# A four-layer network on one core: where three sets of small steps are issued, and which engine does two steps of layer 0's scan

## The chip, the core and the metric

The kernel runs on one core of one Trainium2 chip. It is launched once for a whole forward pass. The metric is device time in microseconds (us), the median of the timed runs. Beside it stands one execution taken by the hardware profiler, with a record for each instruction of the tensor engine (PE, with its weight loads as PEld), the vector engine (DVE), the scalar engine (ACT), GpSimd (POOL) and for the DMA issues of SyncE (SP).

## What is computed

The input is four images of 96 channels, 128 x 128 pixels, in float32. Four layers follow each other, each with a group normalisation ahead of it and its input added behind it:

```python
x = x + _L0_conv_ref(_gn(x), ...)   # conv, two selective scans (forward and backward), layer norm, gate, projection
x = x + _L1_conv_ref(_gn(x), ...)   # local conv, fractional Fourier and FFT branches, 3x3 conv
x = x + _L2_conv_ref(_gn(x), ...)   # deformable 3x3 conv (gathers)
x = x + _L3_conv_ref(_gn(x), ...)   # DCT, layer norm, four Mamba blocks of 16 states, inverse DCT
```

In layer 0 each of the two scans runs over the 16,384 pixels as `h = exp(delta*A)*h + delta*B*u` and gives `y = C*h + D*u`. The results of both directions are added; the sum is normalised over its 96 channels (mean taken off, divided by the root of the mean square), multiplied by a gate and projected. In layer 3 every quadrant of the transformed image goes through the same kind of recurrence with 16 states for each of 192 inner channels.

## The kernel before, in words

The program goes through the samples in phases (`tile_net_kernel`, loop over `b` from -1 to 4, lines 2053 to 2070). A phase has two lanes of work, `front` of sample b+1 (layers 0 and 1 and the offsets of layer 2) and `back` of sample b (the gathers of layer 2 and the head of layer 3), and the inverse transform of sample b-1 beside the front. After them stands `layer3(b)` alone, the Mamba scans. So the profile has one front alone (0 to about 1,630 us), three pairs of a mixed phase and a layer 3, a phase with the back and the inverse alone, and the last layer 3.

Front and back are recorded by a planner (`Program`, line 238). It lists each lane's operations, plans them with rough costs, and issues them so that the two lanes advance in proportion to their plans. While a lane is in layer 0's scan its plan is compressed (`self.program.pace = 0.1`, line 688), so that the other lane does little then. Layer 3 has a planner of its own (`Order`, line 419): an operation is added with an engine, a cost, a key and the operations that it follows; the planner takes the earliest start and, among those that could start within 0.12 us of it, the lowest key. Either way each engine's instructions end in one fixed order (`InOrder`, line 56, ties them), and each engine works through its list strictly in that order. The lists record nearly all operations through one helper, so the profile puts them at L66 (L403 for DMAs), and the reader goes by the names of the tiles (the first letters of a layer's prefix and the digit are cut: `l0_ct` and `l3_ct` are both `l_ct`).

DMAs are issued by SP, one after the other, each where its wait ends. GpSimd issues the gathers of layer 2 (`DMA_INDIRECT l_g<-quad_d,l_i`).

The start. `scan_constants` (line 1540) is called ahead of everything. It loads layer 3's vectors (`l3_vec`) and decay logs (`l3_Alog` into `al`, eight partitions by 16 states to a DMA), then makes `al = -exp(al)`, two columns `rest` and a selection matrix `pick`. Layer 0 then loads its weights and the image in eight pieces (`l0_xt`, line 628) for the normalisation's statistics, and convolves block by block.

Layer 0's scan (`scan`, line 692). A step is a tile of 96 x 512 in one direction k. Steps go forward and backward in turn, n from 0 to 31 for each direction. In the first half (n < 16) a step ends with its `C*h` stored to `part_d`. In the second half the other direction's part is loaded (`part`), and the step goes on (line 754 on): three matmuls into `pm` (the skip term `uc`, `part`, `h`, each through the centring matrix), ACT squares `pm` into `sq` and copies it into `ct`, PE averages the squares into `pv`, ACT makes the inverse root, DVE multiplies, ACT applies the affine, DVE multiplies by the gate, PE projects into `po`, DVE adds the input and takes statistics. `pm`, `pv` and `po` share two PSUM banks (tag "a"). Ahead of all that GpSimd multiplies `du` by the step size `dl`, the only thing that it does in a step.

Layer 3 (`layer3`, line 1503). Two quadrants side by side make a half (`qh` 0 and 1); each half has eight tiles of 512 pixels, so there are 16 tiles i, and each tile has 48 recurrences (`DB` multiplies on DVE, `SC` scans on DVE, `HC` multiplies on GpSimd, ...). `pick2`, a second selection matrix, is filled by two DVE instructions ahead of the planner. For the first tile of a half `pair_head` (line 1638) adds eight operations `weights0` to `weights7`: the generator `pair_weights` (line 1583) issues 34 weight DMAs on SP and prepares them on DVE (`wc` by `win`, copies into `wx`, the split of `wdt` into `wh` and `wl`). The tile's own data (`xc`, DMA from `xd_d`) is loaded by the operation `load`, which follows `weights7`. Then come the layer norm (`pm`, `sub`, `sq`, `pv`, `ln`, `root`, `mul`, `aff`), the convolution (`pu`), the gate (`pz`), the projection (`pb`) and the recurrences. The weights of the second half have nothing to wait for, so the planner issues them right behind those of the first.

Of the kernel before, what the change touches and what calls it, by code (L numbers as in the profile page):

```python
# [23 lines left out]
F32 = mybir.dt.float32  # L24
# [22 lines left out]
def lanes(ap, n):  # L47

    return ap.unsqueeze(2).to_broadcast([ap.shape[0], ap.shape[1], n])
# [452 lines left out]
class Net:  # L502
# [107 lines left out]
    def layer0(self, xin, T, beside):  # L610
# [3 lines left out]
        with self.program.pool(name="l0w", bufs=1) as wp, self.program.pool(name="l0p", bufs=1, space=PSUM) as ps:  # L614
# [74 lines left out]
            with self.program.pool(name="l0b", bufs=3) as wb:  # L689
                edges = [None, None]  # L690

                def scan(k, n):
# [62 lines left out]
                    nc.tensor.matmul(out=pm, lhsT=center[:, 1, :], rhs=uc, start=True, stop=False)  # L755
                    nc.tensor.matmul(out=pm, lhsT=center[:, 0, :], rhs=part, start=False, stop=False)
                    nc.tensor.matmul(out=pm, lhsT=center[:, 0, :], rhs=h, start=False, stop=True)
                    yield
                    ct = wb.tile([C, CH], F32, name="l0_ct", tag="ct")
                    sq = wb.tile([C, CH], F32, name="cn_s", tag="sq")  # L760
                    nc.scalar.activation(sq, pm, AF.Square)
                    nc.scalar.copy(ct, pm)
                    yield
                    pv = ps.tile([C, CH], F32, name="cn_v", tag="a", bufs=2)
# [738 lines left out]
    def layer3(self, T):  # L1503
        tc, nc = self.tc, self.nc
        T.yd_d = self.plane("yd_d")
        with tc.tile_pool(name="l3w", bufs=1) as wp, tc.tile_pool(name="l3q", bufs=2) as wq, tc.tile_pool(
            name="l3p", bufs=2, space=PSUM
        ) as ps, tc.tile_pool(name="l3b", bufs=2) as wb:
            self.pick2 = wp.tile([128, 32, 2, 64], F32R, name="pick2")
            for q in range(2):  # L1510
                nc.vector.tensor_tensor(
                    self.pick2[:, :, q, :],
                    lanes(self.ident[:, 32 * q : 32 * q + 32], 64),
                    lanes(self.ident[:, 64 + 32 * q : 96 + 32 * q], 64),
                    ALU.add,
                )
# [23 lines left out]
    def scan_constants(self, pool):  # L1540


        nc, a = self.nc, self.a
        self.al = pool.tile([128, 2, 3, DS], F32, name="l3_al")
        self.vec = pool.tile([128, 2, 3, 3], F32, name="l3_vec")
        for qh in range(2):
            for j in range(3):
                for q, p, n, m, c in self.inner_parts(j):
                    nc.sync.dma_start(
                        out=self.vec[p : p + n, qh, j, :], in_=a["l3_vec"][c : c + n, 2 * qh + q, m, :]  # L1550
                    )
                    for i in range(0, n, 8):
                        g = (m * C + c + i) // 8
                        nc.sync.dma_start(
                            out=self.al[p + i : p + i + 8, qh, j, :],
                            in_=a["l3_Alog"][2 * qh + q][:, g].rearrange("(e s) -> e s", s=DS),
                        )
        al = self.al.rearrange("p h j s -> p (h j s)")
        nc.scalar.activation(al, al, AF.Exp)
        nc.vector.tensor_scalar_mul(al, al, -1.0)  # L1560


        self.rest = pool.tile([64, 2], F32, name="rest")
        nc.vector.memset(self.rest[:, 0:1], 1.0)
        nc.vector.memset(self.rest[:, 1:2], 0.0)
        for r in (12, 44):
            nc.sync.dma_start(out=self.rest[r : r + 12, 1:2], in_=a["k_ones"][0:12, 0:1])
        nc.vector.tensor_tensor(
            self.rest[:, 0:1], self.rest[:, 0:1], self.rest[:, 1:2], ALU.subtract
        )  # L1570
        self.pick = pool.tile([128, 64], F32R, name="pick")
        nc.vector.tensor_tensor(self.pick, self.ident[:, 0:64], self.ident[:, 64:128], ALU.add)
# [10 lines left out]
    def pair_weights(self, qh, wq):  # L1583
# [7 lines left out]
        wo = wq.tile([128, 3, C], F32, name="l3_wo", tag="wo")  # L1591
        wdt = wq.tile([64, 3, 128], F32, name="l3_wdt", tag="wdt", bufs=1)
        nc.gpsimd.memset(wdt, 0.0)
        for q in range(2):
            nc.sync.dma_start(out=win[:, q, :], in_=a["l3_winT"][2 * qh + q][:, 0 : 2 * C])
            nc.sync.dma_start(out=wz[:, q, :], in_=a["l3_winT"][2 * qh + q][:, 2 * C : 4 * C])
            nc.sync.dma_start(
                out=wc[:, q], in_=a["l3_cwT"][2 * qh + q].unsqueeze(0).to_broadcast([C, 4, 2 * C])
            )
        for j in range(3):  # L1600
            for q, p, n, m, c in self.inner_parts(j):
                nc.sync.dma_start(out=xp[p : p + n, j, :], in_=a["l3_xpT"][2 * qh + q][c : c + n, m, :])
                nc.sync.dma_start(out=wo[p : p + n, j, :], in_=a["l3_woT"][2 * qh + q][c : c + n, m, :])
# [6 lines left out]
        yield 3.0  # L1610
        for q in range(2):
            nc.vector.tensor_tensor(
                wc[:, q], wc[:, q], win[:, q].unsqueeze(1).to_broadcast([C, 4, 2 * C]), ALU.mult
            )
            yield 1.0

        wx = wq.tile([128, 3, 96], F32, name="l3_wx", tag="wx")
        nc.gpsimd.memset(wx, 0.0)
        for j in range(3):
            for q, p, n, _ in self.PARTS[j]:  # L1620
                nc.vector.tensor_copy(wx[p : p + n, j, 32 * q : 32 * q + 32], xp[p : p + n, j, R6:])
                for d in range(2):
                    o = 64 + 12 * d + R6 * q
                    nc.vector.tensor_copy(wx[p : p + n, j, o : o + R6], xp[p : p + n, j, 0:R6])
            yield 0.5

# [5 lines left out]
        nc.vector.tensor_tensor(wl, wdt, whf, ALU.subtract)  # L1632
        yield 1.0
        nc.vector.tensor_scalar(wl, wl, self.rest[:, 1:2], 0.0, ALU.mult, ALU.add)
# [3 lines left out]
    def pair_head(self, i, at, T, before, wq, wb, ps, order):  # L1638
# [11 lines left out]
        T.px = slice(qh * HW * W + t * 2 * CH, qh * HW * W + (t + 1) * 2 * CH)  # L1650
        if t == 0:
            weights = self.pair_weights(qh, wq)

            def more():
                T.wts = next(weights)

            T.wts = None
            for k in range(8):
                o("DVE", 1.0, more, f"weights{k}", after=[f"weights{k - 1}"] if k else [])

        def load():
# [10 lines left out]

        o("DVE", 0.2, load, "load", after=["weights7"] if t == 0 else [],
          others=([last.ops["aff1"]] if last else []) + used("pz2", 2) + used("out", 3))

        def norm(h):
# [47 lines left out]
        norm(1)  # L1724
        ready = ["aff0", "aff1"]
        v = SimpleNamespace(pu={}, pz={})
# [76 lines left out]
        def bc_low():  # L1803
            nc.vector.tensor_tensor(T.bc[64:128, :], v.pb[0:64, :], T.bc[0:64, :].bitcast(F32), ALU.subtract)

        for j in range(3):
            o("PE", 0.9, partial(proj, j), f"pb{j}", after=["silu"] if j == 0 else [f"pb{j - 1}"],
              opens="pb" if j == 0 else None)
# [93 lines left out]
    def pair_scans(self, xd_d, yd_d, wq, wb, ps):  # L1902
# [13 lines left out]

        carry = {}

        def scans(i, T):
# [7 lines left out]
            for n in range(48 * i, 48 * i + 48):  # L1927
# [55 lines left out]
                free = lambda k: ("E", n - k)  # L1983
                pC = main("PC", n, "PE", 0.36, pc, -5.2, (H("bc"), 0), ("PC", n - 1), ("CS", n - 1))
                dA = main("DA", n, "ACT", 0.69, da, -5.1, (H(f"dl{j}"), 0), ("DA", n - 1), ("SC", n - AHEAD))
                main("CS", n, "ACT", 0.58, cs, -5.0, ("PC", n), ("CS", n - 1), ("HC", n - AHEAD))
                pB = main("PB", n, "PE", 0.36, pb, -1000.0, (H("bc"), 0), ("PB", n - 1), ("DB", n - 2))
                dB = main("DB", n, "DVE", 0.62, db, 0.0, ("PB", n), (H(f"du{j}"), 0), ("DB", n - 1), ("SC", n - 2))
# [25 lines left out]

        both(0)
        for i in range(len(tiles)):
            scans(i, parts[i])
            if i + 1 < len(tiles):
                both(i + 1)
# [4 lines left out]
def kernel(ctx: ExitStack, tc: tile.TileContext, a: dict, out: bass.AP):  # L2024
# [5 lines left out]
    net.constants(const)  # L2030
    net.scan_constants(const)
    program = net.program
    net.smalls = [program.pool(f"small{lane}", 1) for lane in range(2)]
# [19 lines left out]
    for b in range(-1, n + 1):  # L2053
# [13 lines left out]
        program.end()  # L2067
        net.nc = net.engines
        if 0 <= b < n:
            net.layer3(samples[b])  # L2070
# [153 lines left out]
```

## Time and profile before

| what | value |
|---|---|
| median of 3 timed runs | 18,809.84 us (18,797.6 to 18,822.2) |
| the profiled execution, whole | 17,757.5 us |
| its span, first to last instruction | 17,755.7 us |
| mean granted PE clock in it | 0.899 |
| busy: PE / DVE / ACT / POOL | 14,126.8 / 12,556.5 / 11,138.5 / 10,731.0 us |
| first image DMA of layer 0 issued | 82.03 us |
| first scan step of layer 0: front alone, then the three mixed phases | 410.1, 2,167.6, 6,408.0, 10,595.9 us |
| last tile of that scan added | 748.8, 2,530.3, 6,753.6, 10,940.4 us |
| first DMA of layer 3 (`l_ln`), four samples | 4,051.8, 8,237.0, 12,423.1, 15,936.2 us |

How to read it: a group's line in the profile gives the engine, the operation and the tiles as output<-inputs, then a count and durations. A line of the timeline gives start and duration in us, merged where equal instructions follow each other; in square brackets stands how long the engine was idle before it and what ended that. In a table of windows each engine's busy time in a stretch is followed by its count of instructions, and the last columns are the PE clock, the share of the DMA engines and GB/s. A float32 matmul has two records, one for each pass. An engine's busy time is no bound by itself; what counts is what is late next in the stretch concerned.

### The profile page before, as it was taken

What the parts mean: (1) busy time and instruction counts of PE and PEld (TensorE: products, weight loads), DVE (VectorE), ACT (ScalarE), POOL (GpSimd) and SP (SyncE); (2) the same over time, 40 slices, a digit from 0 to 9 for tenths busy, and PEclk for the clock granted to TensorE, in tenths of its full rate; (3) what the DMA queues carried; (4) which work ended last, traced back from release to release, by engine and by line L of the source; (5) the groups of instructions that cost most, each with busy time, mean ns of one, the idle gap of its engine ahead of it and who ended that gap; (6) DMA issues with size and microseconds to landing.
All of it is one profiled execution on the core that took longest, in us unless ns stands there. A gap on an engine that the chain in (4) does not pass through costs nothing. (4 is left out here: it accounts for less than half of the span.)

```text
span 17755.7 us, 171824 instructions
## 1 busy us (share of the span) xinstructions
PE 14126.8 (80%) x41152; PEld 6431.4 (36%) x41152; DVE 12556.5 (71%) x22642; ACT 11138.5 (63%) x24735; POOL 10731.0 (60%) x9556
## 2 busy tenths in 40 slices
PE   7897887888998787888999788788899842248998
PEld 2263334433333332634333332444333321123333
DVE  1725585677999576567999757567899855558997
ACT  1613675556777576555777567554777656547776
POOL 0102635636888645553888764562788877747887
PEclk9998998989999897988999898898999966579999
DMA  3525656661000757563000476666000165540001
GB/s 80 159 82 162 182 171 185 190 188 37 8 9 7 208 172 210 172 185 118 9 8 8 118 205 180 182 193 185 11 8 8 35 184 159 158 127 6 8 9 48
DMA packets 1189540, 1940.84 MB, mean 109 GB/s; under 512 B 191985, under 2 KB 711601, under 8 KB 1169457
## 3 DMA queue, kind: packets, MB, share of 16 engines
q1 hardware_dynamic: 893616, 1023.60, 19.9%
q0 software_dynamic: 294912, 906.26, 17.6%
q8 instruction: 328, 5.37, 0.1%
q14 instruction: 684, 5.60, 0.1%
HBM read 1473.67 MB, written 455.61 MB: 109 GB/s over the span
## 5 line engine op out<-in xcount | busy, mean ns | idle before, releaser
L66 POOL DMA_INDIRECT l_g<-quad_d,l_i x4608 | 4552.4, 988 | 3454.4 <-issue 1218.2
L66 ACT ACTIVATE l_acc<-l_g,l_v 128x96 f32<-128x96 f32 x9216 | 3170.0, 344 | 2599.8 <-DVE l_part L66 1557.3
L66 POOL TENSOR_TENSOR l_hc<-l_h,l_cs 128x512 f32<-128x512 f32 x3072 | 3854.5, 1274 | 846.3 <-PE l_py L66 271.4
L66 DVE TENSOR_TENSOR_SCAN l_h<-l_dA,l_carry,l_dB 128x512 f32<-128x512 f32 x3072 | 3916.2, 1275 | 165.8 <-ACT l_carry L66 73.9
L66 ACT ACTIVATE l_dA<-l_dl,l_al 128x512 f32<-128x512 f32 x3072 | 2182.9, 722 | 807.5 <-DVE l_h L66 806.7
L66 DVE SCALAR_TENSOR_TENSOR l_sm<-l_g,l_v,l_acc 128x96 f32<-128x96 f32 x4608 | 1408.1, 312 | 1693.4 <-ACT l_acc L66 1552.0
L66 PE MATMUL l_py<-l_hc,ident 128*128 128x512 f32 x4608 | 2386.6, 607 | 20.0 <-POOL l_hc L66 11.6
L66 DVE TENSOR_TENSOR l_dB<-l_du,l_pB 128x512 f32<-128x512 f32 x3072 | 2135.7, 695 | 317.0 <-POOL l_du L66 25.9
L66 PE MATMUL l_pt<-ident,l_sm 128*128 128x128 f32 (+1 forms) x3584 | 793.9, 329 | 1829.3 <-ACT l_acc L66 706.6
L66 PE MATMUL l_pB<-l_bc,pick 128*128 128x512 f32 x3072 | 1774.8, 578 | 561.5 <-DVE l_dB L66 530.4
L66 ACT COPY l_cs<-l_pC 128x512 f32<-128x512 f32 x3072 | 1782.9, 580 | 626.9 <-PE l_pC L66 541.1
L66 DVE SCALAR_TENSOR_TENSOR l_part<-l_g,l_v,l_acc 128x96 f32<-128x96 f32 x4608 | 1428.0, 310 | 1021.2 <-ACT l_acc L66 1009.7
L66 PE MATMUL l_pC<-l_bc,pick 128*128 128x512 f32 x3072 | 1546.7, 503 | 113.6 <-ACT l_cs L66 104.1
L66 PEld LDWEIGHTS l_pt<-ident,l_sm 128*128 128x128 f32 (+1 forms) x3584 | 507.3, 164 | 2459.8 <-ACT l_acc L66 1432.6
L66 PEld LDWEIGHTS l_pB<-l_bc,pick 128*128 128x128 f32 x3072 | 581.1, 189 | 2215.7 <-DVE l_dB L66 2117.7
L66 PE MATMUL l_pc<-rows,l_wc 96*96 96x508 f32 (+2 forms) x2304 | 1101.3, 611 | 5.8 <-DVE rows L66 5.8
L66 PE MATMUL l_p<-rows,l_c 96*96 96x508 f32 (+2 forms) x2304 | 1078.3, 609 | 30.6 <-DMA rows<-cat_d 14.8
L66 POOL TENSOR_TENSOR l_du<-l_du,l_dl 96x512 f32<-96x512 f32 x256 | 329.3, 1287 | 1263.9 <-DVE l_dl L66 841.6
L66 PE MATMUL l_pu<-l_xq,l_wc 96*64 96x512 f32 (+1 forms) x2048 | 1079.1, 617 | 13.6 <-ACT l_xq L66 13.6
L66 PE MATMUL l_pc<-l_sT,l_wk 128*96 128x512 f32 (+1 forms) x1792 | 1005.7, 676 | 53.1 <-ACT l_sT L66 53.1
L66 PEld LDWEIGHTS l_py<-l_hc,ident 128*128 128x128 f32 x4608 | 879.9, 193 | 381.9 <-issue 172.7
L66 POOL TENSOR_TENSOR l_hc<-l_hc 128x512 f32<-128x512 f32 x768 | 978.0, 1273 | 55.2
(253 smaller groups left out, 21354.0 us busy)
## 6 DMA issues: line engine op xcount, KB each, us to landing
quad_d<-l_qt SPq DMA_DIRECT2D x124, 768.0 KB
x<-l_x SPq DMA_DIRECT2D x384, 192.0 KB
l_g<-quad_d,l_i POOLq DMA_INDIRECT x4608
mix<-l_mx SPq DMA_DIRECT2D x256, 256.0 KB
sp_in<-mix SPq DMA_DIRECT2D x256, 256.0 KB
l_uc<-u_d SPq DMA_DIRECT2D x256, 192.0 KB
l_x<-x SPq DMA_DIRECT2D x256, 192.0 KB
l_xs<-x SPq DMA_DIRECT2D x116, 256.0 KB
```

The source lines that it names most:

```text
L66: ins = op(*args, **kw).ins
```

## The change

It has three parts.

1. Layer 0's scan. The matmul of `part` is gone; GpSimd adds `part` to `h`, and one matmul takes the sum. ACT's square of `pm` is gone; GpSimd squares the copy `ct`.
2. The start. The 12 loads of `l3_vec` and 96 of `l3_Alog` are issued by GpSimd instead of SP. `al`, `rest` and `pick` are made in a function of their own, `scan_lines`, called after the first front has been issued.
3. Layer 3's head. `load` comes first; the weights follow it, in six operations instead of eight, their DMAs in another order (`win`, `wc`, `wz`, `xp`, `wdt`, `wo`), and only what needs them waits for them. The second half's weights now follow the second half's `load`. `pick2` is filled by two operations of the planner, which follow `sub0` and `sub1` of the first tile.

```diff
 # layer 0, scan
                     nc.tensor.matmul(out=pm, lhsT=center[:, 1, :], rhs=uc, start=True, stop=False)
-                    nc.tensor.matmul(out=pm, lhsT=center[:, 0, :], rhs=part, start=False, stop=False)
+                    nc.gpsimd.tensor_tensor(h, h, part, ALU.add)
+                    yield
                     nc.tensor.matmul(out=pm, lhsT=center[:, 0, :], rhs=h, start=False, stop=True)
...
-                    nc.scalar.activation(sq, pm, AF.Square)
                     nc.scalar.copy(ct, pm)
+                    nc.gpsimd.tensor_tensor(sq, ct, ct, ALU.mult)
 # scan_constants
-                    nc.sync.dma_start(
+                    self.tc.nc.gpsimd.dma_start(
                         out=self.vec[p : p + n, qh, j, :], in_=a["l3_vec"][c : c + n, 2 * qh + q, m, :]
...
-                        nc.sync.dma_start(
+                        self.tc.nc.gpsimd.dma_start(
                             out=self.al[p + i : p + i + 8, qh, j, :],
...
+    def scan_lines(self, pool):
+        nc, a = self.nc, self.a
         al = self.al.rearrange("p h j s -> p (h j s)")
         nc.scalar.activation(al, al, AF.Exp)
...
 # pair_head
-            for k in range(8):
-                o("DVE", 1.0, more, f"weights{k}", after=[f"weights{k - 1}"] if k else [])
...
-        o("DVE", 0.2, load, "load", after=["weights7"] if t == 0 else [],
+        o("DVE", 0.2, load, "load",
           others=([last.ops["aff1"]] if last else []) + used("pz2", 2) + used("out", 3))
...
+            for k in range(6):
+                o("DVE", 1.0 if k else 0.01, more, f"weights{k}", after=[f"weights{k - 1}"] if k else ["load"])
...
-        ready = ["aff0", "aff1"]
+        ready = ["aff0", "aff1"] + (["weights2"] if t == 0 else [])
...
+        made = ["weights5"] if t == 0 else []
         for j in range(3):
-            o("PE", 0.9, partial(proj, j), f"pb{j}", after=["silu"] if j == 0 else [f"pb{j - 1}"],
+            o("PE", 0.9, partial(proj, j), f"pb{j}", after=["silu"] + made if j == 0 else [f"pb{j - 1}"],
 # pair_scans
+        self.pick2 = wq.tile([128, 32, 2, 64], F32R, name="pick2", bufs=1)
...
+        for q in range(2):
+            S["fill", q] = order.add("DVE", 4.5, partial(fill, q), -30.0 + q, [parts[0].ops[f"sub{q}"]])
 # tile_net_kernel, in the loop over b
         net.nc = net.engines
+        if b < 0:
+            net.scan_lines(lines)
```

In the built program the changed instructions stand as follows. On DVE in layer 3 all of the first half's weight preparation stands between `load`'s memset and `sub0`; the second half's stands among the recurrences, right behind the output of tile 5. On SP most of the second half's weight DMAs stand early, but its 16 of `wdt` stand around the output of tile 5 and the load of tile 8. In layer 0's scan the order on PE is now `cn_v`, `po`, `pC`, `pd`, `pm` twice, `pB` for a step, where it was `cn_v`, `pm` three times, `pd`, `po`, `pB`, `pC`.

More of the change, by code (lines that the diff above doesn't have):

```diff
@@ L1505, in layer3 @@
         T.yd_d = self.plane("yd_d")
-        with tc.tile_pool(name="l3w", bufs=1) as wp, tc.tile_pool(name="l3q", bufs=2) as wq, tc.tile_pool(
+        with tc.tile_pool(name="l3q", bufs=2) as wq, tc.tile_pool(
             name="l3p", bufs=2, space=PSUM
         ) as ps, tc.tile_pool(name="l3b", bufs=2) as wb:
[L1509 to L1516, printed above, removed]
             self.lnv = self.load(wq, self.a["l3_ln"], [C, 2], "l3_ln", 1)
@@ L1592, in pair_weights @@
         wdt = wq.tile([64, 3, 128], F32, name="l3_wdt", tag="wdt", bufs=1)
+        wx = wq.tile([128, 3, 96], F32, name="l3_wx", tag="wx")
         nc.gpsimd.memset(wdt, 0.0)
+        nc.gpsimd.memset(wx, 0.0)
         for q in range(2):
             nc.sync.dma_start(out=win[:, q, :], in_=a["l3_winT"][2 * qh + q][:, 0 : 2 * C])
-            nc.sync.dma_start(out=wz[:, q, :], in_=a["l3_winT"][2 * qh + q][:, 2 * C : 4 * C])
             nc.sync.dma_start(
@@ L1599, in pair_weights @@
             )
+        for q in range(2):
+            nc.sync.dma_start(out=wz[:, q, :], in_=a["l3_winT"][2 * qh + q][:, 2 * C : 4 * C])
         for j in range(3):
@@ L1602, in pair_weights @@
                 nc.sync.dma_start(out=xp[p : p + n, j, :], in_=a["l3_xpT"][2 * qh + q][c : c + n, m, :])
-                nc.sync.dma_start(out=wo[p : p + n, j, :], in_=a["l3_woT"][2 * qh + q][c : c + n, m, :])
+        for j in range(3):
             for q, p, n, ch in self.PARTS[j]:
@@ L1609, in pair_weights @@
                     )
-        yield 3.0
+        for j in range(3):
+            for q, p, n, m, c in self.inner_parts(j):
+                nc.sync.dma_start(out=wo[p : p + n, j, :], in_=a["l3_woT"][2 * qh + q][c : c + n, m, :])
+        yield
         for q in range(2):
@@ L1614, in pair_weights @@
             )
-            yield 1.0
-        wx = wq.tile([128, 3, 96], F32, name="l3_wx", tag="wx")
-        nc.gpsimd.memset(wx, 0.0)
+            yield
         for j in range(3):
@@ L1624, in pair_weights @@
                     nc.vector.tensor_copy(wx[p : p + n, j, o : o + R6], xp[p : p + n, j, 0:R6])
-            yield 0.5
+        yield
         wh = wq.tile([64, 3, 128], F32R, name="l3_wh", tag="wh")
@@ L1632, in pair_weights @@
         nc.vector.tensor_tensor(wl, wdt, whf, ALU.subtract)
-        yield 1.0
+        yield
         nc.vector.tensor_scalar(wl, wl, self.rest[:, 1:2], 0.0, ALU.mult, ALU.add)
@@ L1650, in pair_head @@
         T.px = slice(qh * HW * W + t * 2 * CH, qh * HW * W + (t + 1) * 2 * CH)
[L1651 to L1657, printed above, removed]
-            for k in range(8):
-                o("DVE", 1.0, more, f"weights{k}", after=[f"weights{k - 1}"] if k else [])
         def load():
@@ L1671, in load, with more @@
                 nc.vector.tensor_copy(T.xq[:, :, 0:3], last.xq[:, :, CH : CH + 3])
-        o("DVE", 0.2, load, "load", after=["weights7"] if t == 0 else [],
+        o("DVE", 0.2, load, "load",
           others=([last.ops["aff1"]] if last else []) + used("pz2", 2) + used("out", 3))
+        if t == 0:
+            weights = self.pair_weights(qh, wq)
+            def more():
+                T.wts = next(weights)
+            T.wts = None
+            for k in range(6):
+                o("DVE", 1.0 if k else 0.01, more, f"weights{k}", after=[f"weights{k - 1}"] if k else ["load"])
         def norm(h):
@@ L1917, in pair_scans, with fill @@
         carry = {}
+        self.pick2 = wq.tile([128, 32, 2, 64], F32R, name="pick2", bufs=1)
+        def fill(q):
+            nc.vector.tensor_tensor(
+                self.pick2[:, :, q, :],
+                lanes(self.ident[:, 32 * q : 32 * q + 32], 64),
+                lanes(self.ident[:, 64 + 32 * q : 96 + 32 * q], 64),
+                ALU.add,
+            )
         def scans(i, T):
@@ L1983, in scans @@
                 free = lambda k: ("E", n - k)
[L1984 removed]
+                pC = main("PC", n, "PE", 0.36, pc, -5.2, (H("bc"), 0), ("fill", 0), ("fill", 1), ("PC", n - 1), ("CS", n - 1))
                 dA = main("DA", n, "ACT", 0.69, da, -5.1, (H(f"dl{j}"), 0), ("DA", n - 1), ("SC", n - AHEAD))
                 main("CS", n, "ACT", 0.58, cs, -5.0, ("PC", n), ("CS", n - 1), ("HC", n - AHEAD))
[L1987 removed]
+                pB = main("PB", n, "PE", 0.36, pb, -1000.0, (H("bc"), 0), ("fill", 0), ("fill", 1), ("PB", n - 1), ("DB", n - 2))
                 dB = main("DB", n, "DVE", 0.62, db, 0.0, ("PB", n), (H(f"du{j}"), 0), ("DB", n - 1), ("SC", n - 2))
@@ L2015, in pair_scans @@
         both(0)
+        for q in range(2):
+            S["fill", q] = order.add("DVE", 4.5, partial(fill, q), -30.0 + q, [parts[0].ops[f"sub{q}"]])
         for i in range(len(tiles)):
@@ L2031 @@
     net.scan_constants(const)
+    lines = ctx.enter_context(tc.tile_pool(name="lines", bufs=1))
     program = net.program
```

## The prediction

> **What bounds the kernel now.** I read the busy table and the slices first, then windows of the three stages that the change touches, then their timelines and the groups of the tiles concerned.
>
> ```profile
> PE 14126.8 (80%) x41152; PEld 6431.4 (36%) x41152; DVE 12556.5 (71%) x22642; ACT 11138.5 (63%) x24735; POOL 10731.0 (60%) x9556
> ...
> PEclk9998998989999897988999898898999966579999
> ```
> No engine bounds the whole. So I took the stages one by one, in a table of windows:
>
> ```profile
> core 0: us, PE busy (x) PEld busy (x) DVE busy (x) ACT busy (x) POOL busy (x), PEclk, DMA share, GB/s
> ...
> 530.00:735.00 205.00, 204.59 (x476) 76.95 (x474) 188.01 (x234) 179.98 (x329) 38.09 (x30) 1.00 0.45 133
> 2300.00:2525.00 225.00, 221.35 (x525) 83.31 (x523) 206.33 (x295) 200.57 (x395) 59.76 (x49) 1.00 0.48 139
> 4440.00:5700.00 1260.00, 1139.09 (x2804) 464.45 (x2803) 1158.59 (x1278) 969.83 (x1708) 1067.12 (x857) 0.99 0.03 8
> ```
> First row: the second half of layer 0's scan in the front alone. PE has no gap (204.59 of 205), DVE is 92% busy, GpSimd 19%. Last row: layer 3's recurrences; DVE is idle 101 us of 1,260, and of these only 47 lie outside its own issue gaps, by the list of its waits, so what is put on DVE there lengthens the stage. The start is bound by SP, which issues small loads ahead of the image:
>
> ```profile
> 3.06 8.73 SPq L1554 DMA_DIRECT2D l_al<-in_l_Alog  x12
> ...
> 69.47 8.52 SPq L1554 DMA_DIRECT2D l_al<-in_l_Alog  x12
> ...
> 82.03 21.43 SPq L403 DMA_DIRECT2D l_xt<-in_x  x8
> ...
> 88.13 2.47 DVE L66 BATCH_NORM_STATS2 stats<-l_xt 96x6 f32<-96x512 f32 x4 [4.06 <-DMA l_xt<-in_x]
> ```
> Layer 3's head is bound by SP as well: `xc` is issued 15.3 us after the first DMA, because 34 weight DMAs stand between, and the normalisation (`cn_y`) starts at +22.7. The offsets agree within 0.4 us in all four samples.
>
> ```profile
> 4051.79 0.34 SPq L516 DMA_DIRECT2D l_ln<-in_l_ln  x1
> ...
> 4067.06 0.32 SPq L1665 DMA_DIRECT2D l_xc<-xd_d  x1
> 4068.36 0.35 DVE L66 CAST l_wh<-l_wdt 64x384 fp32r<-64x384 f32 x1 [1.64 <-DMA l_wdt<-in_l_dtT]
> ...
> 4074.46 1.27 DVE L66 TENSOR_TENSOR cn_y<-l_xc,cn_m 96x512 f32<-96x512 f32 x2
> ```
>
> **What the skill says.** The Trainium skill, "SBUF — State Buffer", section "Who interferes with whom": a VectorE instruction with two SBUF inputs and a GpSimd instruction that reads SBUF exclude each other, and the loser waits fully. The trace agrees: the same product takes 671 ns when GpSimd rests and 1,442 ns when it falls beside GpSimd's `du`, and `du` itself now and then 2,126 instead of 1,271.
>
> ```profile
> L66 DVE TENSOR_TENSOR l_ct<-l_ct,cn_s x128: 657/671/689, 537.8 to 10934.4; 96x512 f32<-96x512 f32 x128
> L66 DVE TENSOR_TENSOR l_ct<-l_ct,l_z x128: 668/1442/1730, 543.2 to 10937.0; 96x512 f32<-96x512 f32 x128
> ```
> "DMA: Bandwidth & Descriptors", section "SWDGE vs HWDGE vs iDMA": for a plain DMA issued from GpSimd, software on GpSimd writes the descriptors; for SP hardware does. The trace of before has on GpSimd's queue only the indirect gathers, 0.95 us busy and about 0.3 of issue each; a plain one is not shown.
>
> **Part by part: the start.** On SP remain four constants (0.74 to 2.54), seven loads of layer 0 (0.31 to 0.45 each; 78.03 to 80.9 now, 2.9 in all) and then the image: first `l_xt` at about 5.9 instead of 82.03, so -76. Behind it the image's statistics and a convolution with PE full from 120 us on follow in a fixed order, so all of it passes through. GpSimd issues 12 + 96 = 108 DMAs. At the gathers' 0.95 + 0.30 = 1.25 us that is 135 us; its first work is `du`, at 408.8 now and at 333 then. So it is hidden up to 333/108 = 3.1 us each. Below that it costs nothing; at 4 us it delays the first `du` by 100. The small packets share the DMA engines with the image: their 4-byte packets took 9 ns each, against 526 ns for the image's 8 KB; I put 2 us on it, at most 16. So -74 (-76 to -60). `scan_lines` now runs where the first front ends, at about 1,630 us: a table load 1.28 and an exponential 0.28 on ACT, two `rest` DMAs on SP, about 0.7 us on DVE, where DVE waits 11 us for the next image anyway: +1 (0 to 4).
>
> **Layer 3's head, first half.** `xc` goes out at +0.4 us, but on DVE all weight preparation stands ahead of `sub0`, so `sub0` waits for the last `wdt` and not for `xc`. SP's list up to it is `win`, `wc`, `wz`, `xp` and 16 `wdt`; `wo`'s six DMAs come later. By the present spacing (0.42 us) the last is issued at about 4,064.1; 1.35 us to landing, as now (4,067.01 to 4,068.36), gives the cast at 4,065.5, and 2.3 us of splitting puts `sub0` at 4,067.8: -6.6, four times -26. At the least nothing is gained, if `wdt` comes as late as now; at the most about 11 us a head, where `xc`'s own path would bind. `pick2`'s two fills (2 x 2.25 us on DVE) go behind `sub1`, covered by DVE's idle time up to the first recurrence at +53; without it they would cost 4.5 each head.
>
> **Layer 3, second half.** Its weights are prepared in DVE's idle time of the head now. After, they stand among the recurrences behind tile 5's output: `wc` 2 x 0.95, `wx` 1.3, `wh` and `wl` 2.0, so 5.2 us on an engine that is the bound there. Before the cast DVE waits for `wdt`, whose DMAs on SP stand around a load that waits for tile 5's store: by the present step from store to load (4,791.31 to 4,794.36: 3.05), ten issues and 1.35 to landing, the cast comes 7 us after the output where 4 us of work covers it: +3 (0 to 7). Queued behind that wait on DVE are the recurrences, and GpSimd's `hc` and PE behind them. Net +8 (4 to 12), four times +32. Layer 3 in all: +6 (-15 to +25).
>
> **Layer 0's scan, 128 changed steps.** Now a step takes 6.87 us in the front alone: 16 passes of 0.43 on PE, no gap. After, 14 passes: 6.01. Three things eat that. First, on PE `po` now stands directly behind `cn_v` of the next step, and `cn_v` waits for ACT's logarithm of the former one, since both share a bank: about 0.96 us in which PE stands, so 6.97. Second, DVE: 5.63 us of work a step without lock waits, 0.77 for the one wait seen above, about 0.4 of gaps. GpSimd now has three operations of 1.27 in a step (3.81), each reading SBUF, where it had one; DVE has `dl`, both products and the scan (0.6 to 1.27 each) that can meet them. My timetable of a step gives 1.25 us of such waits instead of 0.77, hence about 6.9: still inside. From both sides: PE's saved passes could give -0.86 if nothing else bound, and three full lock waits of 0.77 to 1.15 could give +1.5 to +2.6. Third, GpSimd's add 1.27 and square 1.27 in place of the square on ACT (0.57) and one matmul (0.86) lengthen the drain of a phase's last steps by about 2. I take +0.1 a step in the front alone. In the mixed phases DVE is fuller (up to 24.5 us in 25, against 23.5 to 23.8 in the front alone), so +0.2. Sum: 31 x 0.1 + 2 + 3 x (31 x 0.2 + 2) = +29 (-20 to +90).
>
> **The sum.** -74 + 1 + 6 + 29 = -38 on the profiled execution, 17,757.5 to about 17,720. The median shown, 18,809.84, is 1,052 us (5.9%) above that execution. I can't show why; with PE busy 14,127 us, a PE clock some 7% lower would make it. If so, PE's passes are longer in the timed runs and hide more of DVE's waits: the scan then costs about +12 and the sum is -55. I take -45 for the median: 18,765. About 0.2%, 38 us, is what a measurement of this kernel can tell from no change.
>
> **Rivals.** *Cancelled gains*: lock waits make it +0.35 a step and the second half's weights cost 12: -74 + 1 + (-26 + 48) + (128 x 0.35 + 8) = +2, 18,812. For it: DVE is within 2% of full in parts of the mixed phases. Against: layer 0's first half already runs `du` beside the same DVE work. *Slower, the lock in layer 0's scan*: GpSimd's three operations each meet a two-input DVE instruction, and DVE becomes the bound of a step. With r us per step the sum is -74 + 1 + 6 + 8 + 128 r; it crosses zero at r = 0.46 and +38 at r = 0.75. At r = 1.2 it is +95: 18,905; at 2.6, 19,084. For it: the one operation of today already costs 0.77 in the median step. Against: only the product by `z` meets it, the others do not. *The change doesn't do what it says*: GpSimd's software takes over 3.1 us for a DMA, and the first scan waits; at 4 us the start gives -76 + 100, and the sum is about +60: 18,870. For it: plain DMAs on this queue are not in the trace. Against: a gather of 96 descriptors takes 1.25.
>
> **How the numbers follow.** Forecast 0.50 (18,700 to 18,800), cancelled gains 0.27 (18,800 to 18,840), lock 0.18 (18,850 and more), slow queue 0.05. Of the forecast's 0.50 some 0.04 lies closer than 38 us to no change; so faster 0.46, same 0.32, slower 0.22. The range 18,690 to 18,870 leaves out 0.05 below and 0.15 above.
>
> **What would show it.** Start: first `l_xt` near 6 us, GpSimd's issues over by about 145 us, first scan near 335. Head: `cn_y` at +16. Second half: the interval of 48 recurrences that holds the weights longer by about 8 than now (104). Scan: 6.9 to 7.1 us from one `po` addition to the next, PE with gaps before `cn_v`; over 7.6 means the lock, seen as DVE's `dl`, products or scan longer by 1 us in the median. It is wrong if the issues on GpSimd reach past 333 us, or if the mixed phases, whose lanes are merged anew, move by more than 20 us each for reasons outside these steps.

## The result, and the profile after

| | median, us | runs |
|---|---|---|
| before | 18,805.65 (18,788.1 to 18,822.2) | 12 |
| after | 18,821.69 (18,797.2 to 18,841.8) | 12 |
| after / before | 1.0008, 95% interval 1.0 to 1.0016 | |

Forecast was 18,765; the time came out at 18,822, 16 us above before, where the second case ("cancelled gains", 18,812) stood. The profiled execution of after took 18,830.4 us (span 18,828.5). It can't be set against the profile shown of before (17,757.5) line by line: that one was 1,050 us under the median of its own kernel. The kernel before, profiled again in a condition nearer to that of the timed runs, shows why (run e1 below): the stages with gathers are longer there, layer 3 is not. Three conditions occur in this study: A, the result (before 18,806), B (18,627) and C (17,774, in line with the profile shown of before). What makes them isn't shown: the chip's number on record is 4 for B and for e5 to e8 on C, 14 for e9 to e12 on C, and there is none for A. Differences of times below are taken within one condition. Only the profile of after, from A, stands beside the profile shown of before in the rest of this section; the steps of layer 0's scan and layer 3's intervals, which are compared there, agree between B and C for the kernel before (e1, below).

The busy table of after and its PE clock:

```profile
PE 14384.0 (76%) x40896; PEld 6537.0 (35%) x40896; DVE 12630.7 (67%) x22642; ACT 11111.3 (59%) x24607; POOL 11194.8 (59%) x9920
...
PEclk9898878889998887889999897888999855569999
```
PE has 256 instructions fewer (128 matmuls of two passes), ACT 128 fewer, GpSimd 364 more.

The start, in the timeline of after (start, duration, engine, line, operation, tiles; in brackets idle time before it):

```profile
5.53 1.35 SPq L403 DMA_DIRECT2D l_xt<-in_x  x3
...
13.20 2.47 DVE L66 BATCH_NORM_STATS2 stats<-l_xt 96x6 f32<-96x512 f32 x4 [12.33 <-DMA l_xt<-in_x]
...
91.33 0.60 POOL L1547 DMA_DIRECT2D l_al<-in_l_Alog  x1 [2.57 <-DMA l_al<-in_l_Alog]
```
The image's first load goes out at 5.53 instead of 82.03, and GpSimd's last issue is over at 92 us, long before its first `du` (its multiplication in a scan step) at 335.2.

Layer 3's head, timeline of after:

```profile
4216.20 0.34 SPq L516 DMA_DIRECT2D l_ln<-in_l_ln  x1
4216.64 0.36 SPq L1656 DMA_DIRECT2D l_xc<-xd_d  x1
...
4231.72 0.35 DVE L66 CAST l_wh<-l_wdt 64x384 fp32r<-64x384 f32 x1 [5.13 <-DMA l_wdt<-in_l_dtT]
...
4233.68 1.27 DVE L66 TENSOR_TENSOR cn_y<-l_xc,cn_m 96x512 f32<-96x512 f32 x2
```
`xc` is issued at +0.4 us, the cast comes at +15.5, `cn_y` at +17.5 (+16.2 and +16.1 in the two samples that follow) instead of +22.7: as worked out, the weights decide. The other end of that part, on DVE behind tile 5's output in the same layer 3:

```profile
4948.65 1.27 DVE L66 TENSOR_TENSOR_SCAN l_h<-l_dA,l_carry,l_dB 128x512 f32<-128x512 f32 x1
...
4951.02 0.95 DVE L66 TENSOR_TENSOR l_wc<-l_wc,l_win 96x768 f32<-96x768 f32 x1
...
4951.89 0.95 DVE L66 TENSOR_TENSOR l_wc<-l_wc,l_win 96x768 f32<-96x768 f32 x1
4952.76 6.55 DVE L66 COPY l_wx<-l_xp 128x32 f32<-128x32 f32 x12
4959.23 0.34 DVE L66 CAST l_wh<-l_wdt 64x384 fp32r<-64x384 f32 x1
4959.60 0.55 DVE L66 TENSOR_TENSOR l_wl<-l_wdt,l_wh 64x384 f32<-64x384 f32 x1
4960.08 1.27 DVE L66 TENSOR_TENSOR_SCAN l_h<-l_dA,l_carry,l_dB 128x512 f32<-128x512 f32 x1
```
Between two recurrences that are 2.0 us apart elsewhere stand 9.1 us of weight preparation, and the last two instructions of it cost another 1.0 further on. Most of it is twelve small copies, 6.55 us together. The group of these copies follows for after, and for e11 below, where they stand in the head again (count, min/median/max in ns):

```profile
L66 DVE COPY l_wx<-l_xp x96: 154/165/1272, 4224.7 to 17743.1; 128x6 f32<-128x6 f32 x32, 64x6 f32<-64x6 f32 x32, 128x32 f32<-128x32 f32 x16, 64x32 f32<-64x32 f32 x16
```

```profile
L66 DVE COPY l_wx<-l_xp x96: 153/164/182, 3993.7 to 15905.3; 128x6 f32<-128x6 f32 x32, 64x6 f32<-64x6 f32 x32, 128x32 f32<-128x32 f32 x16, 64x32 f32<-64x32 f32 x16
```
A copy takes 0.16 us, but five of the twelve took 1.2 to 1.3 (in one of the four samples three did, and the twelve took 4.3 us): each stood beside one of GpSimd's `hc` (1.27), which follow each other there. The Trainium skill, "SBUF — State Buffer", section "Who interferes with whom", counts copies in a mode with two ports among what excludes GpSimd, and says that who issues first keeps the ports for its whole instruction. The durations agree; whether these copies are in such a mode, no run here shows.
The interval of 48 recurrences that holds this is 112.9 to 113.5 us in the four samples; it was 102.9 to 103.5.

Layer 0's scan, windows of after at the same distance from the first addition of `po` as those of before (front alone, then first mixed phase):

```profile
core 0: us, PE busy (x) PEld busy (x) DVE busy (x) ACT busy (x) POOL busy (x), PEclk, DMA share, GB/s
459.00:664.00 205.00, 180.67 (x399) 62.56 (x400) 181.31 (x227) 164.82 (x290) 132.87 (x90) 0.99 0.44 127
2289.00:2514.00 225.00, 190.20 (x421) 65.25 (x420) 203.52 (x264) 173.80 (x329) 149.57 (x101) 0.98 0.43 127
```
PE was busy 204.6 of 205 and 221.4 of 225; now 180.7 and 190.2. Nothing else has become full: DVE is no busier than it was (188.0 and 206.3 us before). Yet a step takes 7.02 us in the front alone (6.87 before), and from the first to the last addition a mean of 7.38, 8.29 and 8.28 in the mixed phases (6.69, 6.83, 6.83). So the place that PE left is not filled by another full engine, but by waits. The lock, the mutual exclusion of DVE and GpSimd that the prediction priced, shows in the groups (count, then min/median/max in ns):

```profile
L66 DVE TENSOR_TENSOR l_ct<-l_ct,cn_s x128: 669/677/2042, 467.5 to 11492.6; 96x512 f32<-96x512 f32 x128
...
L66 DVE TENSOR_TENSOR l_ct<-l_ct,l_z x128: 669/849/3057, 473.0 to 11495.0; 96x512 f32<-96x512 f32 x128
...
L66 POOL TENSOR_TENSOR l_h<-l_h,l_part x128: 1261/2128/2190, 456.1 to 11466.4; 96x512 f32<-96x512 f32 x128
```
It falls on GpSimd's side: the add takes 2,128 ns in the median where it can take 1,261; DVE's product by `z` even got shorter (1,442 to 849).

### The profile page after: what moved, and what is told of

Read it like the earlier page. It is cut to its first block, busy times and chain, and to the rows that moved or that the text cites. A ratio compares the mean times of both kernels' runs of the same rounds, so it can differ in the third digit from the quotient of the medians.

```text
span 18828.5 us, 171704 instructions
## 1 busy us (share of the span) xinstructions
PE 14384.0 (76%) x40896; PEld 6537.0 (35%) x40896; DVE 12630.7 (67%) x22642; ACT 11111.3 (59%) x24607; POOL 11194.8 (59%) x9920
## 5 line engine op out<-in xcount | busy, mean ns | idle before, releaser
L66 PE MATMUL l_p<-rows,l_c 96*96 96x508 f32 (+2 forms) x2304 | 1132.8, 635 | 19.4 <-issue 13.3
L66 PEld LDWEIGHTS l_pC<-l_bc,pick 128*128 128x128 f32 x3072 | 585.2, 190 | 1022.1 <-ACT l_cs L66 698.3
```

The costliest lines, as they stand in the source:

```text
L66: ins = op(*args, **kw).ins
```

## The experiments

**One part at a time (B).** Each is the kernel before with one part of the diff; e1 is the kernel before itself.

e1: 

> The kernel before, unchanged, timed against itself and profiled beside the single parts. Ratio 1.000 within 0.1%: this is what the comparison makes of no change. If the profile shown of before was one execution in better conditions, this profile is near 18,800 us, with its extra 1,050 us where GpSimd gathers and the DMA engines are busy (phases with the back lane) and not in layer 3 alone (1,736 us a sample). If instead a profiled execution is always quicker than a timed one, it is near 17,760.

e2, part 2: 

> Part 2 of the change alone: layer 3's constants issued by GpSimd, the rest of them after the first front. My theory: the first image DMA is issued 76 us earlier, and all of it passes through: -72 us in the median (-60 to -80), ratio 0.9962. Rival: the time is given back at the end of the first front or in the first mixed phase (small packets, table loads), and less than 40 us is left.

e3, part 3: 

> Part 3 alone: layer 3's tile load ahead of the weights, the second half's weights among the recurrences. From the trace of the changed kernel I expect +7 us for each of four samples: the first scan 6 us earlier, the tiles with the second half's weights 10 to 15 us longer. So +28 us in the median (+20 to +40), ratio 1.0015. Rival: the head's gain and the later loss cancel as I had written (+6, -15 to +25).

e4, part 1: 

> Part 1 alone: GpSimd adds part to h and squares ct in layer 0's scan. My theory now: GpSimd's and DVE's lock makes each of 128 steps longer; the trace of the changed kernel shows 6.78 us a step in the front alone where it was 6.37, and 7.4 to 8.3 in the mixed phases. So about +60 us in the median (+40 to +90), ratio 1.0032, which with -72 and +28 gives the +16 measured. Rival: the steps' loss is given back behind the scan, since the other lane's work moves with it, and this part is within 15 us of nothing; then part 3 or a lost part of the start's gain must make up the rest.

| | ratio (95%) | us | first scan of layer 0 | mean step, front alone / mixed phases | layer 3: first recurrence after its first DMA; 7th interval |
|---|---|---|---|---|---|
| e1 before | 1.0 (0.9991 to 1.0008) | | 410.0 | 6.38 / 6.69, 6.83, 6.84 | 68.8 to 70.1; 102.9 to 103.5 |
| e2 start | 0.9963 (0.9949 to 0.9976) | -72 | 337.9 | 6.37 / 6.69, 6.83, 6.83 | |
| e3 head | 1.0023 (1.0014 to 1.0033) | +34 | 408.9 | 6.38 / 6.69, 6.83, 6.84 | 63.4 to 64.0; 113.3 to 113.9 |
| e4 scan | 1.0047 (1.0033 to 1.0061) | +68 | 410.8 | 6.72 / 7.38, 8.28, 8.21 | |

(The mean step runs over the 31 intervals from the first to the last `po` addition, so it contains the quick last steps.) The start gives what it should and nothing of it is given back. Part 3 costs, part 1 costs more; -72 + 34 + 68 = +30, against +16 measured on A. The profile of e1 spans 18,632 us with layer 3 alone at some 1,737 us a sample, as in the profile shown of before; the last phase with gathers, which no part touches, takes 2,073 us instead of 1,776. There a gather is issued every 1.60 us instead of 1.34 (1.65 on A). So what separates the conditions sits in the gathers' stages. PE's clock is a small part of it: in that last phase PE was busy 684 us at a mean granted clock of 0.62, against 652 at 0.65, which is 33 of the 296 us.

**What makes the mixed steps long (C).** PE's list of waits in the same stretch (6,800 to 6,990 us), e1 and then e4 (engine, tile, what ended the wait: us in total, times, longest):

```profile
PE l_po L66 <- ACT cn_s L66: 3.2, 5, 0.9
```

```profile
PE l_po L66 <- ACT cn_s L66: 26.7, 22, 3.2
PE l_pC L66 <- DVE l_h L66: 9.6, 9, 2.7
```
PE stands at `po` until ACT has taken the logarithm of `cn_v`, since in the built program `po` takes `cn_v`'s bank. There are three theories of why the mixed steps get so long. L: the lock makes the step's instructions themselves longer. Q: what the step gives to GpSimd queues there behind the gathers. S, formed after e6: PE has too few other matmuls between `cn_v` and `po` (its slack) to cover ACT's delays, and passes them on.

e5, only the square on GpSimd: 

> Of part 1 the square alone: GpSimd squares ct, the matmul of part stays. Theory Q (GpSimd's queue: in the mixed phases each operation of the step that is given to GpSimd stands behind the gathers, 1.25 us each, and the chain from pm to po lengthens): front alone unchanged at 6.87 us a step, since 16 passes hide it; mixed phases 7.1 to 7.6 instead of 6.7 to 6.83; +25 to +45 us in the median. Theory L (the lock between GpSimd's add and the recurrence on DVE): the square reads one tile and meets little, so mixed steps stay under 7.0 and the median within 15 us of before.

e6, only the add: 

> Of part 1 the add alone (written just ahead of the pm matmuls): GpSimd adds part to h, ACT keeps the square of pm. Q: like the square, mixed steps 7.1 to 7.6, +25 to +45 us. L: nearly the whole loss of part 1, mixed steps 7.3 to 8.3, +50 to +70 us, and the add's median near 2.1 us as in part 1 (1.26 where it is alone).

```diff
+                    nc.gpsimd.tensor_tensor(h, h, part, ALU.add)
+                    yield
                     pm = ps.tile([C, CH], F32, name="l0_pm", tag="a", bufs=2)
...
-                    nc.tensor.matmul(out=pm, lhsT=center[:, 0, :], rhs=part, start=False, stop=False)
```

e7, part 1 without gathers in the scan: 

> Part 1, and the plan of the scan's lane compressed a hundred times more, so that the gathers and their sums are kept out of layer 0's scan. Q: without gathers in GpSimd's queue the mixed phases' steps fall from 7.4-8.3 to that of the front alone, 7.0 to 7.1; the add still takes 2.1 us. L: the lock is there with or without gathers, and the mixed steps stay over 7.4. The median is not the point (the gathers that are put off come later).

```diff
-            self.program.pace = 0.1
+            self.program.pace = 0.001
```

e8, part 1 with four `ct`: 

> Part 1 with four buffers for ct instead of three. In the trace of part 1 a ct tile lives from ACT's copy to po's end 22.8 us in the mixed phase, which is three steps of 7.6, and the copy waits for po. Theory R (the ring of three tiles closes the loop): a fourth lets the mixed steps fall below 7.4, and at least 25 of part 1's 68 us come back. Rival: the wait is only the last in a chain, the copies start earlier and wait elsewhere, and the steps stay within 0.2 us.

```diff
-                    ct = wb.tile([C, CH], F32, name="l0_ct", tag="ct")
+                    ct = wb.tile([C, CH], F32, name="l0_ct", tag="ct", bufs=4)
```

e9, e6 with a short add: 

> The add alone as in the run before, in the same order of all instructions, but GpSimd adds only the first 60 of 512 columns; the rest of the other direction's part is left out of the sum. So GpSimd's 2.1 us with the lock become some 0.3. Theory S (slack on PE: po follows two matmuls behind cn_v and waits for ACT's logarithm of it; the gathers' sums delay ACT, and PE, no longer full, passes each delay on): the mixed steps stay at 7.3 to 7.8. Theory Q or L (GpSimd's queue, or the lock): they fall to 6.6 to 7.0.

```diff
-                    nc.gpsimd.tensor_tensor(h, h, part, ALU.add)
+                    nc.gpsimd.tensor_tensor(h[:, :60], h[:, :60], part[:, :60], ALU.add)
```
(The planner's cost of it was left at that of 512 columns.)

e10, e6 with `po` later: 

> The add alone again, without the extra turn of the generator behind it. In the built program PE's order is then cn_v, pm, pm, pd, po: po stands three matmuls behind cn_v instead of two, everything that GpSimd does is the same. S: the mixed steps shorten from 7.4-7.8 to 7.0-7.5 and at least a third of the 105 us comes back; the front alone stays at 6.6 or less. Q or L: steps within 0.15 us of the former.

```diff
                     nc.gpsimd.tensor_tensor(h, h, part, ALU.add)
-                    yield
```

e12, the changed kernel on C: 

> The changed kernel beside the others on the same chip. If the three parts add up as they did one by one (-72, +34 and +68), it is +30 us, ratio 1.0016; on the chip of the result it was 1.0008 (1.0 to 1.0016).

All on C. "Slack" is the number of PE passes (0.43 us each) between `cn_v` and `po`, read from the trace in the front alone; "mixed phases" is the sum of the three, each from its first image load to layer 3's first DMA, against the profile shown of before (2,419, 2,443 and 2,443 us).

| | on GpSimd | slack | steady step, front alone | mean step, mixed phases | mixed phases, us | median, ratio (95%) |
|---|---|---|---|---|---|---|
| before | `du` | 8 | 6.87 | 6.69, 6.83, 6.83 | 0 | |
| e5 | + square | 6 | 6.91 | 7.66, 7.51, 7.53 | +16 | +18, 1.0011 (1.0004 to 1.0017) |
| e10 | + add | 6 | 6.96 | 7.10, 7.41, 7.52 | +68 | +54, 1.0032 (1.002 to 1.0044) |
| e9 | + add of 60 | 4 | 6.62 | 7.40, 7.62, 7.51 | +102 | +81, 1.0048 (1.0035 to 1.0062) |
| e6 | + add | 4 | 6.62 | 7.44, 7.80, 7.81 | +116 | +105, 1.0062 (1.0048 to 1.0076) |
| e8 | + both | 0 | 7.02 | 7.09, 7.71, 7.68 | +192 | +183, 1.0103 (1.0087 to 1.0118) |
| e12, all parts | + both | 0 | 7.02 | 7.36, 8.24, 8.24 | +189 | +149, 1.0085 (1.0071 to 1.0098) |
| e7 | + both | 0 | 7.02 | 6.69, 6.87, 6.89 | +47 | +59, 1.0035 (1.0022 to 1.0049) |

e7 settles the first question: with the gathers' lane kept out (the gathers, their sums and what follows them), a mixed step is exactly that of the front alone, 7.02 (the means lie lower for the quick last steps), while the add still takes 2.18 us. So the lock alone doesn't make the mixed steps long, and my L falls. (The kernel before was not run with this pace, so what e7's own +47 and +59 consist of stays open.) e5 and e6 both miss their bands: the square cost less than Q had it (+18), the add far more than either (+105). e11 below, which leaves the scan alone, has +14 in the column of mixed phases, so e5's +16 there can't be told from none. e9 tells S from Q: GpSimd's add is shorter by half and 77% of the loss stays, with GpSimd idle for about 3 us ahead of most adds in the stretch looked at. In e10 GpSimd has the same work as in e6, `po` stands one matmul later on PE, and half of the loss is gone. That half isn't shown to be the slack's alone, for the edit also moved other instructions: in e10 the recurrence stands right behind the statistics on DVE, and in the front alone the logarithm ends 3.2 us behind `cn_v`, where it was 2.0 in e6. A piece of e6 shows one such delay on its way through the engines:

```profile
6716.65 2.04 DVE L66 TENSOR_TENSOR l_ct<-l_ct,cn_s 96x512 f32<-96x512 f32 x1
...
6716.86 1.27 POOL L66 TENSOR_TENSOR l_du<-l_du,l_dl 96x512 f32<-96x512 f32 x1
...
6717.47 1.02 PE L66 MATMUL l_pm<-l_h,l_center 96*96 96x512 f32 x2
...
6719.21 0.30 DVE L66 SCALAR_TENSOR_TENSOR l_sm<-l_g,l_v,l_acc 128x96 f32<-128x96 f32 x1
...
6719.55 0.34 ACT L66 ACTIVATE l_acc<-l_g,l_v 128x96 f32<-128x96 f32 x1 [3.46 <-DVE l_sm L66]
...
6722.29 0.67 ACT L66 ACTIVATE cn_s<-cn_v,eps 96x512 f32<-96x512 f32 x1
...
6723.01 2.02 PE L66 MATMUL l_po<-l_ct,l_woT 96*96 96x512 f32 x2 [4.52 <-ACT cn_s L66]
...
6724.82 1.91 PE L66 MATMUL l_pC<-l_uc,l_wbc 96*96 96x512 f32 x2
```
A product on DVE meets `du` and takes 2.04 instead of 0.68; the gather's sum `sm` behind it on DVE is late; ACT, in order, waits 3.46 us at the next part of that sum (`acc`), of which the lock's 1.36 are the smaller part; the logarithm stands behind that; and PE stands 4.5 us at `po`. In the kernel before the same delays meet 3.4 us of matmuls between `cn_v` and `po`. The traces show both sides of this. In 24 steps of the second mixed phase the logarithm ends 2.4 to 4.8 us behind `cn_v` in e1, 3.2 in the mean, and there `po` would stand 3.3 us behind `cn_v` anyway; in e6 it ends after 1.4 to 6.2 us, again 3.2 in the mean, and only 1.6 us are covered. So S holds for the waits that the add brings. For the square it is not the whole: in e5 PE's longest wait is at `cn_v` for GpSimd's square (9.0 us in 190), which is Q's place, at a small price.

The waits are not all of it, for PE's clock falls behind them. The second half of layer 0's scan in the second mixed phase, e1 and then e4:

```profile
core 0: us, PE busy (x) PEld busy (x) DVE busy (x) ACT busy (x) POOL busy (x), PEclk, DMA share, GB/s
6785.00:6995.00 210.00, 201.49 (x477) 74.75 (x475) 190.95 (x288) 183.66 (x365) 64.04 (x53) 1.00 0.52 151
...
6780.00:7030.00 250.00, 202.27 (x419) 68.49 (x418) 202.05 (x290) 172.63 (x338) 152.86 (x111) 0.91 0.43 127
```
In e4 PE is busy as long for 419 passes as in e1 for 477. The record of the granted clock shows stretches at 0.5. In e6's steps of this phase there are seven of them, 3.4 or 6.8 us long, and each begins 2.3 to 3.8 us after PE began a wait of 2.2 to 4.5 us at `po`. The one in the piece above runs from 6,721.2 to 6,728.0: two passes that took 1.02 us ahead of it (`pm`) take 1.91 in it (`pC`). The steps of 7.02 us, where PE waits 0.8 at a time, have none. So a long wait is followed by slower passes, which lengthen the step further. How much they add is an estimate: e12's steps in this phase take 255 us together, those of e7 213; of the 43 us between them 22 are idle time of PE and 21 busy time, and 16 more passes of 0.43 make only 7 of these. That leaves a third of the 43 to the clock. No run holds the clock fixed, so its share stays open.

e8 refutes the ring of `ct` tiles as a price: the steps did get shorter by 0.3 to 0.6, but the three mixed phases are as long as those of e12 (+192, +189). Fewer gathers' sums lay among these steps (24 instead of 32 in the second and third mixed phase), so more were left for behind the scan. So a mean step of a mixed phase is no measure by itself; the phase is.

e12 missed its figure by far: +149 on C, where the sum from B was +30 and A gave +16. Its parts in the profile, against the one shown of before: first front -60 (-72 start, +12 scan and `scan_lines`), mixed phases +189, layer 3 +24, the last gathers +1; together +154 of 157. On B part 1 alone made the mixed phases 44 us longer (e4 against e1; e2 and e3, which leave the scan alone, give -2 and -11 in this sum), on C e12's are 189 longer. Part 1's price thus differs with the condition (a gather every 1.34 or 1.60 us); that slow gathers give back what the scan loses fits these numbers, but no run shows it alone, and it stays open. A bank of its own for `cn_v`, which would take away the reason for `po`'s wait, wasn't tried.

**A better version (C).** Parts 2 and 3 without part 1, and the second half's weights freed again:

e11: 

> Parts 2 and 3 without part 1, and the second half's weights no longer follow the second half's load, so that they are prepared in DVE's idle time of the first tile. Theory: -72 us from the start, and -6 for each of four heads with nothing lost in the middle of layer 3 (the seventh interval of 48 recurrences back at 103 us): -95 us, ratio 0.9947. Rival: the second half's weights get in the way of the first tile in the head, and what part 3 gained there is gone: -72, ratio 0.996.

```diff
-                o("DVE", 1.0 if k else 0.01, more, f"weights{k}", after=[f"weights{k - 1}"] if k else ["load"])
+                o("DVE", 1.0 if k else 0.01, more, f"weights{k}", after=[f"weights{k - 1}"] if k else ["load"] * (i == 0))
```
Measured: 17,694.8 us, -78, ratio 0.9954 (0.994 to 0.9967): the fastest of all. The seventh interval is 103.3 to 103.7 again and the first recurrence stays early (63.6 to 64.4), but the eighth and ninth intervals together are 2.3 to 2.8 us longer (why was not looked into), so layer 3 gains 3 us a sample, not 6.

## Why the prediction was right or wrong, step by step

- *Start, -74*: right. The first image load at 5.5, the first scan 72 us earlier, -72 in the median. GpSimd's issues took 0.84 us each (108 in 91 us), below the gathers' 1.25 that I took, so the cover up to `du` was never in question. (My rival case took a gather for 96 descriptors; the profile of before has 294,912 packets on that queue for 4,608 gathers, 64 each.) `scan_lines`, +1: the first front of e11 ends 72 us earlier, the scan in it 73; right.
- *Layer 3's head, first half, -6.6*: right in mechanism; `cn_y` 5.2 to 6.2 earlier, the first recurrence 5 to 6.
- *Second half, +8*: right in mechanism, mis-sized. The term that failed is "`wx` 1.3": that is what twelve copies take in the head, where GpSimd rests; among the recurrences they meet its `hc` and took 4.3 us in e3, 6.6 in after (4.3 in one sample). I had looked for the lock in layer 0 only. The wait for `wdt` was 1.2 to 1.7 us in e3, none where the copies took longer. I had 3, by a sum that doesn't come out: 3.05, ten issues of 0.42 and 1.35 are 8.6 us, not 7. The seventh interval grew by 10.3, the next two by some 2.6 together. Layer 3 in all: +6 predicted, +34 measured (e3; its profile gives 6 to 8 a sample, some 28).
- *Layer 0's scan, front alone, +0.1 a step*: right: 7.02 where I had 6.97, and PE stands 0.77 us a step at `po`, for the reason named. The drain was too small: the first front is 12 us longer in e4 where I had +5. My sum for DVE left out the 0.4 us of gaps that it names (with them 7.28, over 6.97); that did no harm, since the lock falls on GpSimd's side and DVE is busy 181 of 205 us.
- *The mixed phases, +0.2 a step*: this failed. I priced them as the front alone with a fuller DVE and took PE's wait at `po` for a fixed 0.96. In fact DVE never became the bound; the longest wait was 3.2 us in e4 and 4.5 in e6, because the gathers' sums stand ahead of the logarithm on ACT and DVE, and because PE, no longer full, passes on such delays. I counted the passes saved and not what they had covered. Behind the long waits PE's clock was halved as well, a term that the prediction doesn't have. 25 us became +44 (B) and +189 (C). My upper end of +90 for the scan in all was too low for C. My sign for the lock, steps over 7.6, came true without it: DVE's products stayed at medians of 677 and 849 ns in after.
- *The lock as the slower case*: the lock is there, but the three GpSimd operations don't make DVE the bound. It lengthens GpSimd's add, and DVE's products only now and then; its part in the loss is that it starts some of the delays that PE then passes on.
- *The clock*: wrong. The 5.9% between profile and median was put down to PE's clock, and 7 us of the forecast rest on it (-45 instead of -38). On C the kernel before takes 17,774 us in its timed runs too, and PE-bound steps are 6.87 us in B and C alike. On A the kernel before has no profile; the change's steps in the front alone are 7.02 on A, B and C.

The median lies in the range through the second case, and near it by luck: the condition decided, and on C the same kernel is 0.85% slower.

## What to carry to other kernels

A full engine covers what the others do; before taking work from it, look for what it will wait for next, and how many of its instructions stand between a producer on another engine and the wait. That slack must be judged in the stage where the other engines' queues are most mixed, not in the cleanest one, and a gain or loss there is read from the whole phase. Where PE is the engine, read its granted clock beside its waits: here the passes behind a long wait were slower. A set-up step freed from an early point should not be allowed to drift onto the engine that is full later.

## What the runs showed of the hardware

How dear the lock is for small instructions: the loser waits to the end of the other's, whatever its own length. Beside the copies above, in e9 the add of 60 columns takes 299 ns at the least, but 1,166 in the median, since it starts beside the recurrence and ends 0.1 us behind it (the group, then two lines of its timelines):

```profile
L66 POOL TENSOR_TENSOR l_h<-l_h,l_part x128: 299/1166/1237, 530.6 to 11009.7; 96x60 f32<-96x60 f32 x128
```

```profile
602.17 1.27 DVE L66 TENSOR_TENSOR_SCAN l_h<-l_dA,l_e,l_du 96x512 f32<-96x512 f32 x1
602.38 1.17 POOL L66 TENSOR_TENSOR l_h<-l_h,l_part 96x60 f32<-96x60 f32 x1 [3.50 <-PE cn_v L66]
```
PE's granted clock fell to half for 3.4 or 6.8 us at a time behind waits of 2.2 to 4.5 us (seven times in e6's second mixed phase), and not in steps with waits of 0.8 us.

Gathers' pace differed by 19 and 23% between the conditions (1.34, 1.60 and 1.65 us each in a phase that no kernel here changed), while stages without them agreed within 0.2%.
